# A graph layer on one core: only the source table is made ahead of the edge loop, and node sums move into one tile per batch

## The chip, the cores and the metric

The kernel runs on one core of a Trainium2 chip. The metric is the device time of one execution in microseconds (us); smaller is better. Times of one profiled execution and times of three executions without the profile are given separately, since they differ here.

## The reference

A graph has N = 6250 nodes with 128 features each and E = 100000 edges with 4 attributes each. The edges are sorted by destination. For every edge a small network makes a message; the messages are added up per destination node; a second network updates the nodes; two normalizations follow.

```python
msg_in = concat([x[src], x[dst], edge_attr], axis=1)         # E x 260
h = silu(msg_in @ mW1 + mb1)                                  # E x 128
messages = h @ mW2 + mb2
aggregated = segment_sum(messages, dst, num_segments=N)       # N x 128
u = silu(concat([x, aggregated], axis=1) @ uW1 + ub1)
y = x + (u @ uW2 + ub2)
z = x + (layer_norm(y) * ln_g + ln_b)
out = (z - mean(z)) / sqrt(var(z) + 1e-5)                     # N x 128, float32
```

## The kernel before, in words

**The algebra.** `mW1` has three parts: for the source's features, for the destination's, and for the attributes. The kernel makes two tables in device memory: `tab_a` = x times the first part, `tab_b` = x times the second part plus `mb1`. For an edge it then only needs a row of `tab_a`, a row of `tab_b` and the product of its attributes. Since `h @ mW2` is linear, the kernel adds up `h` itself per node (`acc`, turned: 128 features on the partitions, nodes along the columns) and counts the edges per node (`deg`). The products with `mW2` and with the second part of `uW1` are merged into one matrix `wc` and one row `bc_row` (`merged`).

**The edge loop.** The 100000 edges are cut into 98 groups of 1024, that is eight tiles of 128 edges (the last has six). For group `g`:

- `fetch(g + 4)` issues eight gathers on GpSimd (L159). Each brings 128 rows of `tab_a`, chosen by a list of sources, into a tile `ga`; six such tiles exist. The first five groups (`RAW = 5`) gather from x itself, since `tab_a` is not there yet; for them TensorE turns the rows and multiplies them with the weight in the loop.
- `load(g + 3)` issues three loads on SyncE's queue: the destinations, copied to as many partitions as the window has nodes (`near`, L298), the window of `tab_b` that starts at the group's first destination (`mv`, L414), and the attributes (`st`, L415). The start of the window is a register value.
- `hidden(g)`: VectorE adds `ga` and the product `pre` (L470); ScalarE takes silu into `h` (L471).
- `matrices(g + 2)`: VectorE makes the two one-hot matrices between edges and the 96 nodes of the window (L423, L433).
- `sums(g)`: TensorE multiplies `h` by the one-hot matrix, eight tiles into one PSUM tile `pt` (L479).
- `before_rows(g + 2)`: TensorE makes `pre` out of `mv` and `st` (L455).
- `add(g)`: VectorE adds the 96 columns to `acc` and `deg` at a register's column (L485).

**The nodes.** There are 49 tiles of 128 nodes, in 13 batches of up to four. Because the edges are sorted, a batch's sums are complete some groups after its own. `node_stage` therefore lays the work of one batch over three groups: `node_u` (TensorE, L505 to L507; ScalarE, L509), `node_y` (TensorE, L518 and L519; VectorE, L521 with moments L498 and L499), and `inverse`, `node_z`, `node_o` (ScalarE, L526 and L535; VectorE, L527 to L550; the store, L559). Batch 11 is treated as a whole at group 96, and batch 12, with one tile, after the loop.

**The start.** All of x is loaded into `x_sb`. `turned` (TensorE L319, ScalarE L320) turns a batch into `xT`; `product` multiplies it with both parts of the weight at once (TensorE, L329), ScalarE copies the half for `tab_a` (L331, store L332), VectorE adds `mb1` to the half for `tab_b` (L334, store L335). Between two batches the code places the lists: `destination_lists` turns the destinations and finds each group's first one, and checks that every group fits into its window; if one does not, a general path (`general`, `update`) does the whole work again after the loop. `source_lists` turns the sources into columns for the gathers.

**Order.** The order of instructions on each engine is the order of the code (`manual_schedule`). Waits between engines come from tiles: a new tile of a pool waits until the old tile in its buffer was read.

Of the kernel before, what the change touches and what calls it, by code (L numbers as in the profile page):

```python
# [24 lines left out]
def kernel(  # L25
# [28 lines left out]
    W = 96  # L54
    NW = NP + W
    K1 = W + ED
# [10 lines left out]
    BN = 4  # L67
    NB = -(-NT // BN)
# [3 lines left out]
    assert NG - 2 == (NB - 2) * G + G and NG % RB == 0 and EC * NC == E and EJ * EQ == EC and SQ * SK == NG * G  # L72
# [7 lines left out]
    def tiles_of(g):  # L80
        return min(G, TI - g * G)

# [11 lines left out]
    ps1 = edges.enter_context(tc.tile_pool(name="one_ps", bufs=1, space=PSUM))  # L94

# [3 lines left out]
    def narrow():  # L99
        return ps.tile([P, 2 * P], F32, name="pt")  # L100

    src_l = work.tile([P, GE], I32, name="near")[:SQ, : SK * P].rearrange("q (k c) -> q k c", c=P)
# [3 lines left out]
    x_sb = consts.tile([P, NT, H], F32, name="x_sb")  # L106
    nf = N // P
    w1 = consts.tile([P, 2, H], F32, name="w1")

    def load_x(eng, i0, n):  # L110
        eng.dma_start(
            x_sb[:, i0 : i0 + n, :], x[i0 * P : (i0 + n) * P].rearrange("(i p) c -> p i c", p=P)
        )

    load_x(nc.scalar, 0, 4)
    load_x(nc.sync, 4, 4)
    nc.scalar.dma_start(w1, mW1[: 2 * H].rearrange("(s k) f -> k s f", k=P))
    load_x(nc.sync, 8, 8)
    load_x(nc.scalar, 16, 8)
    load_x(nc.sync, 24, 8)  # L120
    load_x(nc.scalar, 32, 8)
    load_x(nc.sync, 40, nf - 40)
# [3 lines left out]
    w_row_i = consts.tile([P, W], I32, name="w_row_i")  # L126
    nc.gpsimd.iota(w_row_i, pattern=[[1, W]], base=0, channel_multiplier=0)
    p_col_i = consts.tile([P, 1], I32, name="p_col_i")
    nc.gpsimd.iota(p_col_i, pattern=[[0, 1]], base=0, channel_multiplier=1)
    floor_i = consts.tile([1, NB * G], I32, name="floor_i")  # L130
    nc.gpsimd.iota(floor_i, pattern=[[BN * P, NB], [0, G]], base=0, channel_multiplier=0)
# [4 lines left out]
    def source_lists(k0, k1):  # L136
        n = k1 - k0
        src_n = work.tile([P, GE], F32, name="s")[:SQ, : SK * P].rearrange("q (k c) -> q k c", c=P)
        nc.vector.tensor_copy(src_n[:, :n], src_l[:, k0:k1])
        pt = wide()  # L140
        for k in range(n):
            nc.tensor.transpose(pt[:, k, :SQ], src_n[:, k, :], ident[:SQ, :SQ])
        nc.vector.tensor_copy(
            src_s[:, k0 * SQ : k1 * SQ].rearrange("c (k q) -> c k q", q=SQ), pt[:, :n, :SQ]
        )
# [20 lines left out]
    for g in range(RAW):  # L166
        fetch(g)

    if N % P:
        nc.vector.memset(x_sb[:, nf, :], 0.0)  # L170
        nc.sync.dma_start(x_sb[: N - nf * P, nf, :], x[nf * P :])
    nc.vector.memset(src_l[:, SK - 1, :], 0)
    kf = (nf_e - SQ) // SQ
    nc.sync.dma_start(
        src_l[:, 1 : 1 + kf, :],
        src[SQ * P : (1 + kf) * SQ * P].rearrange("(k p c) -> p k c", p=SQ, c=P),
    )
    q0 = nf_e - (1 + kf) * SQ
    if q0:
        nc.sync.dma_start(  # L180
            src_l[:q0, SK - 1, :],
            src[(1 + kf) * SQ * P : nf_e * P].rearrange("(p c) -> p c", c=P),
        )
    if E % P:
        nc.sync.dma_start(
            src_l[q0 : q0 + 1, SK - 1, : E - nf_e * P],
            src[nf_e * P :].rearrange("(o c) -> o c", o=1),
        )
    b1 = bcast("b1", mb1)

    dst_l = work.tile([P, GE], I32, name="near")
# [14 lines left out]
    mv = []  # L206
    for k in range(NM):
        t = consts.tile([K1, H], F32, name=f"mv{k}")
        nc.sync.dma_start(t[W:], mW1[2 * H :])
        mv.append(t)  # L210

    const_ps = ps1.tile([P, W], F32, name="w_row")
    nc.vector.tensor_copy(const_ps, w_row_i)
    w_row = const_ps
# [8 lines left out]

    acc = consts.tile([P, NW], F32, name="acc")
    deg = consts.tile([1, NW], F32, name="deg")
    deg_g = consts.tile([W, NG], F32, name="deg_g")

    def clear():
        for i0, n in groups(NW, NW // 4):
            nc.scalar.copy(acc[:, i0 : i0 + n], zero.to_broadcast([P, n]))  # L230
            nc.scalar.copy(deg[:, i0 : i0 + n], zero[0:1].to_broadcast([1, n]))
# [3 lines left out]
    base_i = consts.tile([1, NG], I32, name="base_i")  # L235
    bad_i = consts.tile([1, 1], I32, name="bad_i")
# [6 lines left out]
    def destination_lists():  # L243
        base_c = work.tile([NG, 1], F32, name="base_c", bufs=1)
        nc.vector.tensor_copy(base_c, dst_l[:, 0:1])
        rel_n = work.tile([P, GE], F32, name="s")[:NG]
# [5 lines left out]
        base_f = work.tile([1, NG], F32, name="base_f", bufs=1)  # L252
        row = to_row(base_c, NG)
        nc.vector.tensor_copy(base_f, row)
        nc.vector.tensor_copy(base_i, row)
        p_b = narrow()
        nc.tensor.matmul(p_b[:, :NG], ones[0:1, :], base_f, start=True, stop=True)
        nc.vector.tensor_scalar(base_p, p_b[:, :NG], p_col, None, op0=OP.add)

        far = work.tile([NG, 2], F32, name="far", bufs=1)  # L260
# [6 lines left out]
        worst = work.tile([1, 2], F32, name="worst", bufs=1)  # L267
        nc.vector.tensor_reduce(worst[:, 0:1], to_row(far[:, 0:1], NG), AX.X, OP.max)
        nc.vector.tensor_scalar(worst[:, 0:1], worst[:, 0:1], -mid * mid, None, op0=OP.add)
        early = work.tile([1, NG], F32, name="early", bufs=1)  # L270
        nc.vector.tensor_copy(early, floor_i[:, :NG])
        nc.vector.tensor_sub(early[:, : NG - 1], early[:, : NG - 1], base_f[:, 1:])
        nc.vector.tensor_reduce(worst[:, 1:2], early[:, : NG - 1], AX.X, OP.max)
# [29 lines left out]
    xT = consts.tile([P, NP], F32, name="xT")  # L303

# [3 lines left out]
    if True:  # L308
        zeros = node.tile([W, H], F32, name="y", bufs=1)
        nc.vector.memset(zeros, 0.0)  # L310
        pad = node.tile([ED, NG * GE - E], F32, name="uT", bufs=1)
        nc.vector.memset(pad, 0.0)
        parts = groups(NT, BN)

        def turned(k):
            i0, n = parts[k]
            pt = wide()
            for i in range(n):
                nc.tensor.transpose(pt[:, i, :], x_sb[:, i0 + i, :], ident)  # L319
            nc.scalar.copy(  # L320
                xT[:, i0 * P : (i0 + n) * P], pt[:, :n, :].rearrange("p i f -> p (i f)")
            )

        def product(k):
            i0, n = parts[k]
            pm = wide().rearrange("p i f -> p (i f)").rearrange("p (i s f) -> p i s f", s=2, f=H)
            for i in range(n):
                cols = slice((i0 + i) * P, (i0 + i + 1) * P)
                nc.tensor.matmul(pm[:, i], xT[:, cols], w1, start=True, stop=True)  # L329
            ta = work.tile([P, G, H], F32, name="s")  # L330
            nc.scalar.copy(ta[:, :n], pm[:, :n, 0])  # L331
            nc.sync.dma_start(by_node(tab_a)[:, i0 : i0 + n, :], ta[:, :n])  # L332
            tb = node.tile([P, BN, H], F32, name="o")
            nc.vector.tensor_add(tb[:, :n], pm[:, :n, 1], b1[:, None, :].to_broadcast([P, n, H]))  # L334
            nc.sync.dma_start(by_node(tab_b)[:, i0 : i0 + n, :], tb[:, :n])  # L335

        turned(0)
        for k in range(len(parts)):
            if k + 1 < len(parts):
                turned(k + 1)  # L340
            product(k)
            if k == 3:
                attributes(0)
            if k == 5:
                destination_lists()
# [236 lines left out]
    for g in range(NG):  # L582
        if g == 3:
            weights()
        if g == 6:
            merged()
# [281 lines left out]
```

## Time and profile before

| what | us |
|---|---|
| median of three executions | 1401.74 (1395.29 to 1404.93) |
| the profiled execution | 1054.17 |
| its span, from the first to the last instruction | 1052.3 |
| GpSimd (POOL) busy in it | 739.4 |
| TensorE (PE) busy | 685.3 |
| VectorE (DVE) busy | 458.5 |
| ScalarE (ACT) busy | 227.3 |

The mean clock that TensorE was granted in the span was 0.734 of full speed. The profile comes from one execution. Its page has the busy time of each engine, a picture of the span in 40 slices, and the costliest groups of instructions. A line such as "L159 POOL DMA_INDIRECT ga<-tab_a,src_i x742 | 700.1, 944 | 250.2 <-issue 206.3" reads: line 159, on POOL, an indirect transfer into the tile `ga`, 742 times, 700.1 us in sum, 944 ns each; POOL stood idle for 250.2 us just ahead of them, of which 206.3 without any wait that the profile shows. PEld is TensorE's weight load. SPq and ACTq are the queues on which SyncE and ScalarE issue transfers.

### The profile page before, as it was taken

The page shows a single profiled execution, that of the slowest core. Times are in us where ns is not written, and L with a number is a line of the kernel's source. Part 1 is how long each engine was busy: PE and PEld are TensorE (multiplying, and loading weights), DVE is VectorE, ACT ScalarE, POOL GpSimd, SP SyncE. Part 2 cuts the span into 40 slices and gives each one's busy share as a digit, 9 for nine tenths or more (in the row PEclk, how much of TensorE's full clock was granted, in tenths as well). Part 3 has the DMA queues.
Part 4 walks back from the last instruction along what each step waited for, and adds up shares of the span by engine and source line. Part 5 has one row for each costly group of instructions (what it writes and reads, how often), then busy time and mean ns, then how long its engine had stood idle before and what let it go on. Part 6 is the DMA issues. An engine that isn't in the chain of part 4 may idle for free. (4 is left out here: it accounts for less than half of the span.)

```text
span 1052.3 us, 11528 instructions
## 1 busy us (share of the span) xinstructions
PE 685.3 (65%) x3791; PEld 605.0 (57%) x3791; DVE 458.5 (44%) x913; ACT 227.3 (22%) x298; POOL 739.4 (70%) x791
## 2 busy tenths in 40 slices
PE   3667884876765775775675575675676675676652
PEld 2447864755755655755665555665566665556631
DVE  1325444736346345335335445435435435335312
ACT  1144112222122122122113122112112112113022
POOL 6707777777777777777777777777777777777710
PEclk7798995977677668668678676667866677766555
DMA  8555542525324324334324325324424433324200
GB/s 214 167 168 139 142 129 75 153 78 145 105 71 139 112 70 134 95 95 132 112 71 139 104 71 145 101 74 127 110 84 129 106 88 116 105 88 116 66 22 15
DMA packets 80699, 114.49 MB, mean 109 GB/s; under 512 B 20791, under 2 KB 58222, under 8 KB 80632
## 3 DMA queue, kind: packets, MB, share of 16 engines
q1 hardware_dynamic: 52728, 60.94, 19.8%
q0 software_dynamic: 25024, 51.30, 17.9%
q10 hardware_dynamic: 2880, 1.44, 0.5%
q8 instruction: 32, 0.52, 0.2%
q14 instruction: 35, 0.29, 0.1%
HBM read 102.34 MB, written 11.28 MB: 108 GB/s over the span
## 5 line engine op out<-in xcount | busy, mean ns | idle before, releaser
L159 POOL DMA_INDIRECT ga<-tab_a,src_i x742 | 700.1, 944 | 250.2 <-issue 206.3
L479 PE MATMUL pt<-oh,h 128*128 128x96 f32 x1564 | 292.0, 363 | 313.0 <-ACT h L471 307.2
L479 PEld LDWEIGHTS pt<-oh,h 128*128 128x128 f32 x1564 | 271.4, 269 | 344.6 <-ACT h L471 337.4
L455 PE MATMUL pre<-mv,st 100*128 100x128 f32 x1564 | 266.3, 337 | 6.6 <-DVE s L446 6.6
L455 PEld LDWEIGHTS pre<-mv,st 100*128 100x128 f32 x1564 | 256.0, 253 | 6.8 <-DVE s L446 6.8
L471 ACT ACTIVATE h<-s 128x1024 f32<-128x1024 f32 (+1 forms) x93 | 98.0, 1053 | 563.4 <-DVE s L470 559.4
L470 DVE TENSOR_TENSOR s<-ga,pre 128x1024 f32<-128x1024 f32 (+1 forms) x93 | 113.3, 1218 | 161.4 <-DMA ga<-tab_a,src_i 152.8
L485 DVE TENSOR_TENSOR acc<-acc,pt 128x96 f32 x98 | 24.9, 254 | 251.1 <-PE pt L479 242.6
L423 DVE TENSOR_SCALAR_CACHE_REDUCE st<-near,base_p 96x1024 f32<-96x1024 int32 x98 | 124.4, 1269 | 3.3 <-issue 3.0
L433 DVE TENSOR_TENSOR oh<-w_row,rel 128x768 f32<-128x768 f32 x98 | 92.8, 947 | 0.0
L159 POOL DMA_INDIRECT ga<-in_x_dram,src_i x40 | 38.1, 953 | 14.3 <-issue 11.9
L521 DVE TENSOR_TENSOR y<-pn,x_sb 128x512 f32<-128x512 f32 (+1 forms) x13 | 8.6, 661 | 79.4 <-PE pn L519 79.4
L329 PE MATMUL pre<-w,xT 128*128 128x256 f32 x98 | 29.7, 457 | 7.3 <-ACT xT L320 5.8
L509 ACT ACTIVATE uT<-pn,ub_col 128x512 f32<-128x512 f32 (+1 forms) x13 | 8.6, 662 | 113.5 <-PE pn L507 113.5
L535 ACT ACTIVATE pn<-y,r 128x128 f32<-128x128 f32 x49 | 22.6, 461 | 35.5 <-DVE r L528 34.3
L334 DVE TENSOR_TENSOR o<-pre,b 128x512 f32<-128x512 f32 (+1 forms) x13 | 8.4, 659 | 48.0 <-ACT s L331 30.6
L329 PEld LDWEIGHTS pre<-w,xT 128*128 128x128 f32 x98 | 21.4, 229 | 13.5 <-ACT xT L320 8.3
L519 PE MATMUL pn<-u,uT 128*128 128x128 f32 x98 | 26.7, 359 | 0.0
L518 PE MATMUL pn<-ub_row,ones 1*128 1x128 f32 x98 | 25.6, 343 | 1.2 <-ACT uT L509 1.2
L477 PE MATMUL pt<-ident,deg_g 96*1 96x96 f32 x98 | 26.1, 266 | 0.0
L485 DVE TENSOR_TENSOR deg<-deg,pt 1x96 f32 x98 | 23.0, 235 | 0.2 <-issue 0.2
L518 PEld LDWEIGHTS pn<-ub_row,ones 1*128 1x128 f32 x98 | 15.6, 198 | 9.2 <-ACT uT L509 3.1
(96 smaller groups left out, 352.5 us busy)
## 6 DMA issues: line engine op xcount, KB each, us to landing
near<-in_dst_dram SPq DMA_DIRECT2D x98, 384.0 KB
ga<-tab_a,src_i POOLq DMA_INDIRECT x742
mv<-tab_b SPq DMA_DIRECT2D x98, 48.0 KB
tab_a<-s SPq DMA_DIRECT2D x12, 256.0 KB
tab_b<-o SPq DMA_DIRECT2D x12, 256.0 KB
out_dram<-o SPq DMA_DIRECT2D x12, 256.0 KB
st<-ea_d SPq DMA_DIRECT2D x98, 16.0 KB
ea_l<-in_edge_attr_dram SPq DMA_DIRECT2D x10, 156.2 KB
```

Of the source, the lines that this page charges most:

```text
L159: nc.gpsimd.indirect_dma_start(out=rows[g][:, i, :], out_offset=None, in_=x if g < RAW else tab_a[:, :], in_offset=bass.IndirectOffsetOnAx ...
L329: nc.tensor.matmul(pm[:, i], xT[:, cols], w1, start=True, stop=True)
L423: nc.vector.tensor_scalar(stbuf[g % NST][:W], near.pop(g), base_p[:W, g : g + 1], 0.0, op0=OP.is_equal, op1=OP.add, accum_out=deg_g[:, g : ...
L433: nc.vector.tensor_tensor(oh[g][:, :n], w_row[:, None, :].to_broadcast([P, n, W]), rel[:, g, :n, None].to_broadcast([P, n, W]), op=OP.is_e ...
L455: nc.tensor.matmul(pre[g][:, i, :], st[:, i, :], mv[g % NM], start=True, stop=not raw)
L470: nc.vector.tensor_add(s[:, :n], rows.pop(g)[:, :n], p[:, :n])
L471: nc.scalar.activation(h[:, :n], s[:, :n], AF.Silu)
L477: nc.tensor.transpose(pt[0:1, P : P + W], deg_g[:, g : g + 1], ident[:W, :W])
L479: nc.tensor.matmul(pt[:, :W], h[:, i, :], o[:, i, :], start=i == 0, stop=i == n - 1)
L485: nc.vector.tensor_add(at, at, of)
L518: nc.tensor.matmul(py[:, i, :], ones[0:1, :], ub2_row, start=True, stop=False)
L519: nc.tensor.matmul(py[:, i, :], u[:, i, :], u2, start=False, stop=True)
```

## The change

- Ahead of the loop only `tab_a` is made, and copied by VectorE (`make_a`). The columns of x, the products for `tab_b` and its rows are made batch by batch in the loop (`load_x`, `turned_x`, `make_b` in `node_stage`), each a group apart; only batches 0 and 1 of `tab_b` come ahead of it. x lives in tiles per batch.
- The lists, the tail of the source lists and the loads of the attribute weights are placed behind the making of `tab_a`; `checks` and the rest of the source lists come at group 6.
- The window has 80 nodes, not 96.
- `acc` and `deg` are tiles of 768 columns per batch. `open_batch` copies what reaches into the next batch and zeroes the rest, on ScalarE. A second register gives the column (`offs`).
- The last two batches have three and two tiles, not four and one; their groups are 94 and 97.
- `before_rows` runs one group ahead, before `sums`. The sum of `ga` and `pre` is made in `ga`. `pt` has one PSUM buffer, not two; one bank `pn` serves the nodes, `turned_x` and `make_b`.
- `node_y` adds the bias row in one product of up to 512 columns, not one per tile. The root's table is loaded early for the last batch.

```diff
-    W = 96
+    W = 80
+    AW = 768
...
+    batches = [(BN * k, BN) for k in range(NT // BN - 1)]
+    rest_t = NT - BN * len(batches)
+    batches += [(NT - rest_t, rest_t - 2), (NT - 2, 2)]
+    NB = len(batches)
+    last = [G * k + G for k in range(NB - 2)] + [NG - 4, NG - 1]
...
     def narrow():
-        return ps.tile([P, 2 * P], F32, name="pt")
+        return ps1.tile([P, 2 * P], F32, name="pt")
+
+    def bank():
+        return ps1.tile([P, BN, P], F32, name="pn")
...
+    def turned_x(k, pt, pool, **kw):
+        n = batches[k][1]
+        for i in range(n):
+            nc.tensor.transpose(pt[:, i, :], xs[k][:, i, :], ident)
+        xT[k] = pool.tile([P, BN * P], F32, **kw)
+        nc.scalar.copy(xT[k][:, : n * P], pt[:, :n, :].rearrange("p i f -> p (i f)"))
...
+    def make_b(k):
+        i0, n = batches[k]
+        pm = bank()
+        product(k, 1, pm)
+        tb = node.tile([P, BN, H], F32, name="o")
+        nc.vector.tensor_add(tb[:, :n], pm[:, :n], b1[:, None, :].to_broadcast([P, n, H]))
+        nc.sync.dma_start(by_node(tab_b)[:, i0 : i0 + n, :], tb[:, :n])
+
+    def make_a(k, pm):
+        i0, n = batches[k]
+        product(k, 0, pm)
+        ta = first.tile([P, BN, H], F32, name="ta", bufs=3)
+        nc.vector.tensor_copy(ta[:, :n], pm[:, :n])
+        nc.sync.dma_start(by_node(tab_a)[:, i0 : i0 + n, :], ta[:, :n])
...
+    for k in range(NB):
+        if k + 1 < NB:
+            pt[k + 1] = turned_first(k + 1)
+        make_a(k, pt.pop(k)[:, BN:])
...
+    lists = destination_lists()
+    make_b(0)
+    make_b(1)
...
-        s = work.tile([P, G, H], F32, name="s")
-        nc.vector.tensor_add(s[:, :n], rows.pop(g)[:, :n], p[:, :n])
+        s = rows.pop(g)
+        nc.vector.tensor_add(s[:, :n], s[:, :n], p[:, :n])
         nc.scalar.activation(h[:, :n], s[:, :n], AF.Silu)
...
+    def open_batch(k):
+        acc[k] = node.tile([P, AW], F32, name="acc")
+        deg[k] = node.tile([1, AW], F32, name="deg")
+        c0 = 0
+        if k:
+            width = batches[k - 1][1] * P
+            c0 = AW - width
+            nc.scalar.copy(acc[k][:, :c0], acc[k - 1][:, width:])
+            nc.scalar.copy(deg[k][:, :c0], deg[k - 1][:, width:])
+        nc.scalar.copy(acc[k][:, c0:], zero.to_broadcast([P, AW - c0]))
+        nc.scalar.copy(deg[k][:, c0:], zero[0:1].to_broadcast([1, AW - c0]))
...
     def node_stage(g):
...
+        for k in range(NB - 1):
+            if g == last[k]:
+                node_u(k)
...
+        for k in range(2, NB):
+            if g == G * k - G - 2:
+                load_x(nc.sync, k, node, name="x", bufs=3)
+            if g == G * k - G - 1:
+                turned_x(k, bank(), node, name="xT", bufs=3)
+            if g == G * k - G:
+                make_b(k)
...
         if g == 6:
-            merged()
+            checks(*lists)
+            source_lists(1, SK)
+            start.close()
...
-        pt = sums(g)
-        if g == RAW - 1:
+        if g + 1 >= RAW:
             before_rows(g + 1)
-        if g >= RAW - 1:
-            before_rows(g + 2)
-        add(g, pt)
+        if g == NG - 1:
+            node_x(NB - 1)
+        add(g, sums(g))
         node_stage(g)
```

## The prediction

> **What bounds the kernel now.** I read the page's table of busy time first, then POOL's waits, then the timeline at the head, at a batch in the middle and at the tail. The page's groups give the pace:
>
> ```profile
> PE 685.3 (65%) x3791; PEld 605.0 (57%) x3791; DVE 458.5 (44%) x913; ACT 227.3 (22%) x298; POOL 739.4 (70%) x791
> ...
> L159 POOL DMA_INDIRECT ga<-tab_a,src_i x742 | 700.1, 944 | 250.2 <-issue 206.3
> ```
>
> No engine is full: POOL is busy 70%. But its idle time is mostly "issue", which is no wait. The waits of POOL show how it splits:
>
> ```profile
> POOL ga L159 <- issue: 218.2, 716, 0.3
> POOL ga L159 <- DMA ea_d<-uT: 24.3, 1, 24.3
> POOL ga L159 <- DMA ga<-tab_a,src_i: 12.5, 41, 0.3
> ```
>
> The columns are total, times and longest. Hundreds of pauses of 0.3 us, none longer, and one of 24.3 us. A gather of 128 rows so costs 0.944 + 0.305 = 1.249 us, whatever else runs, and the 782 gathers of the kernel take 782 x 1.249 = 977 us of the 1052.3 us span. Everything in the loop has to beat eight gathers, 10.0 us per group; if it does, it is free. The timeline (start, duration, engine, line) shows the two ends that POOL does not fill:
>
> ```profile
> 4.14 1.11 POOL L159 DMA_INDIRECT ga<-in_x_dram,src_i  x1 [2.38 <-DVE near L172]
> ...
> 53.20 0.94 POOL L159 DMA_INDIRECT ga<-in_x_dram,src_i  x1 [0.30 <-issue]
> ...
> 76.70 0.32 SPq L353 DMA_DIRECT2D ea_d<-uT  x1
> ...
> 78.44 0.94 POOL L159 DMA_INDIRECT ga<-tab_a,src_i  x1 [24.30 <-DMA ea_d<-uT]
> ...
> 1003.45 0.94 POOL L159 DMA_INDIRECT ga<-tab_a,src_i  x1 [0.30 <-issue]
> ...
> 1029.51 0.95 DVE L470 TENSOR_TENSOR s<-ga,pre 128x768 f32<-128x768 f32 x1
> ...
> 1033.28 2.88 PE L479 MATMUL pt<-oh,h 128*128 128x96 f32 x12 [15.13 <-ACT h L471]
> ...
> 1046.46 0.26 SPq L563 DMA_DIRECT2D out_dram<-o  x1
> ```
>
> The 40 gathers from x end at 54.1. The next needs tab_a, whose last write goes out at 75.1, in one queue with tab_b's, so POOL stands until 78.4 (the named ea_d is merely the last DMA of that queue). At the end POOL is done at 1004.4, and 47.9 us follow. The last group's rows are there by about 1007, but its add starts at 1029.5: batch 11 is ahead of it on DVE and ACT.
>
> Is the loop really below 10 us? Windows of 80 us, eight groups each, say so for the busy sums (columns PE, PEld, DVE, ACT, POOL; PE has 48 to 56 of 80 us in three of them):
>
> ```profile
> 564.00:644.00 80.00, 51.27 (x302) 46.07 (x302) 38.35 (x74) 16.29 (x22) 60.45 (x65) 0.76 0.36 104
> ```
>
> At the lower PE clock it is tight. From the tail's rows: sums 3.73, pre 3.67, a small transpose 0.37, so 7.8 per group, 62 per eight; batch matmuls add 6.1 (L505 to L507) and 6.4 (L518, L519): 75 of 80 us.
>
> **What the Trainium skill says.** "Perfetto Trace Analysis", per-instruction lifecycle: a gather's row ends when its descriptors are written, not when data land. It agrees: group 96's last gather ends at 996.9 and its add, which waited for it, starts at 999.4, so landing costs 2.5 us. "DMA: Bandwidth & Descriptors", SWDGE vs HWDGE vs iDMA: cores of GpSimd compute these descriptors in software. The trace agrees, 940 to 961 ns over 742 gathers, so smaller loads elsewhere shall not quicken them. "TensorE: Matmul & The Clock Gate", Part 1: the PE clock is either half or full. The same sums take 2.02 and 3.73 us here. "Runtime: NRT & Kernel Launch", model-switch cost, gives about 70 us for a first execution: no cover for the gap in the next part.
>
> **The two times.** The profiled execution took 1054.2 us, the median of the runs is 1401.7: 347 us that no view shows. If they are a constant around the kernel, an edit's gain carries over unchanged. If each gather is slower without the profile, they are 0.44 us on each of 782. If all is slower alike, it is a factor 1.33. I work in the profiled execution and carry the difference over unchanged, the middle of the three.
>
> **The change, part by part.**
>
> *Head.* Tables are made in 13 steps. Before, a step is four transposes (0.60), four products of 256 columns (1.99) and an ACT copy (0.58): starts 3.2 us apart. Now products have 128 columns (1.0 to 1.7), and one DVE copy (about 0.66) frees the buffer: 2.4 to 3.2 us. Three further costs of before go: b1's late landing (DVE waits 17.4 us, to 23.7), the destination lists between steps 5 and 6 (PE's next transposes start at 48.3 instead of near 40) and source lists (2 us). But the queue of SP carries six x tiles, b1 and three lists ahead of the first tab_a write, and the copy tiles are three deep, so step 3 waits for write 0, issued by my estimate at 18 to 20 us. Then 10 steps x 2.4 to 3.2, and 2.5 to land: tab_a is ready at 45 to 55, against 54.1 when POOL asks, plus two iotas of 0.25. I take 1 us of wait left and 0.6 of iotas: 24.3 - 1.6 = 22.7 gained.
>
> *What is late next.* The lists, tab_b's first two batches and the four mv loads now come after A, and the loop starts behind them. On SP: last tab_a write about 52, src lists and mv loads (these four took 4.3 before) to 57, tab_b to 60, the register load 2.3, mv landed at 65.5. On DVE two matrices (2.2 each) and two copies of 1.2 follow, so the first sums come near 78 to 81, against 89.85 before. Raw groups take 7.6 us each (89.85, 97.44, 105.08), so the activation of group 5 ends near 114 to 118. This matters since it now releases the gather's buffer (the sum is made in place, until now DVE's add released it): six buffers, so gather group 11, due at 54.9 + 60 = 115, waits for it. At g = 6 DVE runs checks and source_lists first (two reduces of 1.21, ten of about 0.2, casts of 0.55 and 0.86, some 7 us), and group 12 waits for that: 0 to 7 us in all, I take 3. Head: 19.7 gained.
>
> *Loop.* Windows of 80: the largest distance inside a group in the reference's dst is 70 nodes and offsets reach 529 of 688, so the general path stays unused. Sums lose 16 of 96 columns (3.73 to 3.1), oh 16% of 0.95, near 64 KB. Added per eight groups: four transposes (1.1 slow), four products (3.3), a DVE add (0.69), one x load and a tab_b write on SP. node_y's four bias matmuls become one of 512 columns (3.2 to 2.07). open_batch is four ACT copies (0.4 to 0.7 each, 2.2) ahead of uT. There is one pn bank, so make_b on PE waits for uT, about 2.7, and behind PE wait pre and the next sums. Slow PE: 8 x 7.2 = 57 + 6.1 + 5.3 + 4.4 + 2.7 = 76 of 80, one more than before. Both hide behind the gathers: zero. Without that cover, one microsecond per batch costs 11. make_b's write also sits in SP's queue ahead of the next near, mv and st; it delays them up to 9 us, and near(g+4) has nearly two groups, so zero.
>
> *Tail.* From POOL's end E (1004.4 there): y of batch 11 (three tiles) delays the add of group 96 from E-5 to E-2.6; activation to E-1.5, sums E+1.7, inverse and z of batch 11 on DVE to E+7. Then group 97: add 0.95, activation 0.9, sums 2.4, add 0.5, two matmuls of 256 columns 2.2, silu 0.5, y 2.8, add and moments 1.5, root and reciprocal 0.9, scaling 1.0, three DVE operations 1.4, moments 1.0, inverse 0.8, scaling 1.0: 17.9, so E+24.9. From the last ACT (1046.4) to the end before: 5.9. Sum 30.8 against 47.9: 17.1 gained. Of this 8 come from batch 11 done sooner, the rest from the shorter queue in front of group 97.
>
> Total 19.7 + 17.1 = 37 us, to a span of 1015; the median becomes 1402 - 37 = 1365.
>
> **Rivals.** *The missing 347 us are in the gathers* (0.20). 40 raw gathers then end at 72, not 54, and only 6 of the 24.3 us were ever waited for; the gain is 5 + 17 = 22, so 1380. For it: gathers are most of the time. Against: their spread is 2%. *Everything is slower alike* (0.08): 37 x 1.33 = 49, 1353. *A still comes late* (0.12): SP's queue and landing x tiles keep tab_a until 70, and the lists' wait comes at 7: gain 24.3 - 16 - 7 + 17 = 18, so 1384. *The batch work makes the loop the bound* (0.10, slower): place, the group where node_u, open_batch, uT and make_b run in turn through one pn bank; PE there waits for ACT and ACT for DVE. Price: what an eight-group stretch takes beyond 80 us, times 11. It decides from 84 on (4 saved, 3.4 break even). If waits of 2 to 3 us come at each of node_u, make_b, node_y and z, 76 becomes 85 to 86, so 11 x 5.5 = 60 - 37: 1425. For it: 76 of 80 at the slow clock. Against: the clock was full in part of every window (0.69 to 0.76 on average).
>
> **How the numbers follow.** The forecast has 0.50 and by its own costs 1350 to 1375. Leaving out the slower rival and the upper edge of the late table gives 1340 to 1395. A measurement here tells about 1% (14 us) from none: faster from 1388 down. Faster: 0.48 + 0.17 + 0.08 + 0.08 = 0.81; same 0.10; slower 0.09.
>
> **What would show it.** Right: POOL's wait for a DMA on tab_a below 5 us, waits for ACT of a few us near 115 to 130, pauses of 0.3 elsewhere, 31 us after the last gather. Wrong: a wait of POOL for ACT in every eighth group, or a gather pitch other than 1.25 us.

## The result, and the profile after

| | median, us | runs |
|---|---|---|
| the kernel before | 1403.34 (1395.29 to 1412.18) | 4 |
| the changed kernel | 1453.05 (1446.99 to 1463.32) | 4 |
| ratio | 1.036, 95% interval 1.027 to 1.045 | |

The forecast was 1365 us with a range of 1340 to 1395. The change is 50 us slower in this comparison instead of 37 us faster.

The profiled execution of the changed kernel took 1463.32 us, and its span 1461.5. So nothing large lies outside of the span here, as it had seemed to in the profile of the kernel before (1054.17 profiled, 1401.74 as median). First the page of the changed kernel: TensorE's busy time, its clock in 40 slices, and two groups (sum and mean of their busy time, then the idle time ahead of them and what ended most of it):

```profile
PE 885.3 (61%) x3858; PEld 777.7 (53%) x3858; DVE 451.3 (31%) x936; ACT 238.8 (16%) x338; POOL 739.3 (51%) x792
...
PEclk9987756556555555555555555555555555555555
...
L181 POOL DMA_INDIRECT ga<-tab_a,src_i x742 | 699.9, 943 | 638.5 <-ACT h L516 372.1
...
L545 DVE TENSOR_TENSOR acc<-acc,pt 128x80 f32 x98 | 23.4, 238 | 733.1 <-remote 504.1
```

The gathers cost what they cost before (943 ns), but POOL now stands for 638.5 us ahead of them, 372.1 of it until ScalarE has read the gather's buffer. The add of the sums (L545) stands 504.1 us for "remote", a release that the profile can put down to no instruction. The waits (total, times, longest) show how few and how long these are:

```profile
ACT h L516 <- DVE ga L515: 541.1, 55, 21.2
DVE acc L545 <- remote: 504.1, 35, 15.5
POOL ga L181 <- ACT h L516: 372.1, 53, 15.6
...
POOL ga L181 <- DMA src_l<-in_src_dram: 38.9, 1, 38.9
```

Thirty-five waits of 14.4 us on average, in 98 groups. And the wait for `tab_a`, which was to fall from 24.3 us to 1.6, is 38.9. Two groups on the timeline (start, duration, engine, line), TensorE first and then the adds of the sums on VectorE:

```profile
751.36 3.70 PE L524 MATMUL pt<-oh,h 128*128 128x80 f32 x16 [2.30 <-ACT h L516]
754.86 3.70 PE L500 MATMUL pre<-mv,st 84*128 84x128 f32 x16
758.35 0.34 PE L522 MATMUL pt<-ident,deg_g 80*1 80x80 f32 x1
758.48 3.62 PE L524 MATMUL pt<-oh,h 128*128 128x80 f32 x16
761.90 3.70 PE L500 MATMUL pre<-mv,st 84*128 84x128 f32 x16
774.62 0.29 PE L522 MATMUL pt<-ident,deg_g 80*1 80x80 f32 x1 [9.02 <-DVE deg L545]
```

```profile
755.10 0.24 DVE L545 TENSOR_TENSOR acc<-acc,pt 128x80 f32 x1 [3.08 <-PE pt L524]
...
774.19 0.24 DVE L545 TENSOR_TENSOR acc<-acc,pt 128x80 f32 x1 [15.41 <-remote]
```

The first group's sums are recorded to 755.06, and VectorE adds them at 755.10. The second group's are recorded to 762.10, but VectorE gets them at 774.19, 12 us later. The semaphore events of the trace say the same: one for the first `pre` at 761.47, where the record ends at 758.56; then one at 774.17 for the second group's sums and one at 774.33 for its `pre`. So the results of 33 instructions took 12.9 us to come, 0.39 us for each on average, and the records give them about 7 us. It is no even pace: the first group's 16 matmuls were done in the 3.7 us that their record says. "Perfetto Trace Analysis" of the Trainium skill, section Tensor Engine Instruction, says that the profiler works out the end of a TensorE instruction from its size and does not observe it. This trace agrees: the end of the second group's sums is 12 us too early, and only whoever waits for the result shows it.

### The profile page after: what moved, and what is told of

Same layout as the page of the kernel before. It is cut to its first block, busy times and chain, and to the rows that moved or that the text cites. A ratio compares the mean times of both kernels' runs of the same rounds, so it can differ in the third digit from the quotient of the medians.

```text
span 1461.5 us, 12138 instructions
## 1 busy us (share of the span) xinstructions
PE 885.3 (61%) x3858; PEld 777.7 (53%) x3858; DVE 451.3 (31%) x936; ACT 238.8 (16%) x338; POOL 739.3 (51%) x792
## 4 chain that ended last, share of the span: by engine, by line
another core or an unknown queue 37%; PE 25%; DVE 16%; issue 12%; ACT 5%; DVEq 2%; DMA 1%; POOL 1%; ACTq 0%; SPq 0%
PE pt L524 12%; PE pre L500 4%; DVE ga L515 4%; DVE st L468 4%; ACT h L516 3%; DVE oh L478 2%; PE pn L569 2%; PE pn L570 2%; ACT pn L597 2%; DVE bn L556 1%; PE pn L328 1%; DVE var L557 1%; PE pre L328 1%; DVEq L515 1%
## 5 line engine op out<-in xcount | busy, mean ns | idle before, releaser
L181 POOL DMA_INDIRECT ga<-tab_a,src_i x742 | 699.9, 943 | 638.5 <-ACT h L516 372.1
L524 PE MATMUL pt<-oh,h 128*128 128x80 f32 x1564 | 348.1, 415 | 174.6 <-ACT h L516 156.8
L524 PEld LDWEIGHTS pt<-oh,h 128*128 128x128 f32 x1564 | 332.8, 323 | 194.9 <-ACT h L516 172.2
L500 PE MATMUL pre<-mv,st 84*128 84x128 f32 x1564 | 351.0, 409 | 23.1 <-issue 22.1
L500 PEld LDWEIGHTS pre<-mv,st 84*128 84x128 f32 x1564 | 332.4, 318 | 28.3 <-issue 27.0
L545 DVE TENSOR_TENSOR acc<-acc,pt 128x80 f32 x98 | 23.4, 238 | 733.1 <-remote 504.1
L516 ACT ACTIVATE h<-ga 128x1024 f32<-128x1024 f32 (+1 forms) x93 | 98.1, 1055 | 726.2 <-DVE ga L515 541.1
L522 PE MATMUL pt<-ident,deg_g 80*1 80x80 f32 x98 | 30.9, 315 | 191.6 <-DVE deg L545 191.6
L468 DVE TENSOR_SCALAR_CACHE_REDUCE st<-near,base_p 80x1024 f32<-80x1024 int32 x98 | 124.3, 1269 | 7.1 <-issue 5.2
L515 DVE TENSOR_TENSOR ga<-ga,pre 128x1024 f32<-128x1024 f32 (+1 forms) x93 | 113.2, 1217 | 26.8 <-issue 22.0
L478 DVE TENSOR_TENSOR oh<-w_row,rel 128x640 f32<-128x640 f32 x98 | 79.8, 814 | 0.0
L569 PE MATMUL pn<-acc,wc 128*128 128x512 f32 (+2 forms) x26 | 24.3, 1037 | 89.2 <-DVE acc L545 89.2
L328 PEld LDWEIGHTS pn<-w,xT 128*128 128x128 f32 x98 | 20.2, 305 | 25.6 <-ACT uT L572 22.7
```

The costliest lines, as they stand in the source:

```text
L181: nc.gpsimd.indirect_dma_start(out=rows[g][:, i, :], out_offset=None, in_=x if g < RAW else tab_a[:, :], in_offset=bass.IndirectOffsetOnAx ...
L328: nc.tensor.matmul(pm[:, i, :], xT[k][:, i * P : (i + 1) * P], w1[:, part, :], start=True, stop=True)
L468: nc.vector.tensor_scalar(stbuf[g % NST][:W], near.pop(g), base_p[:W, g : g + 1], 0.0, op0=OP.is_equal, op1=OP.add, accum_out=deg_g[:, g : ...
L478: nc.vector.tensor_tensor(oh[g][:, :n], w_row[:, None, :].to_broadcast([P, n, W]), rel[:, g, :n, None].to_broadcast([P, n, W]), op=OP.is_e ...
L500: nc.tensor.matmul(pre[g][:, i, :], st[:, i, :], mv[g % NM], start=True, stop=not raw)
L515: nc.vector.tensor_add(s[:, :n], s[:, :n], p[:, :n])
```

## The experiments

The chips on which the runs took place are of two kinds. On kind A (four chips) the kernel before takes 1048 to 1054 us, on kind B (four others) 1394 to 1423, profiled or not. All runs of one chip are compared with runs of the kernel before on the same chip, so ratios are used below, with the kind beside them. In the first comparison the kernel before took 1403 us, kind B. No run shows one of these chips at two different times, so whether the kind belongs to a chip for good or to its state at that hour is not shown.

The theories, as the expectations name them. R: in some executions TensorE's results come late, and this bounds the loop. O: the missing 347 us lie outside of the span or evenly everywhere. Q: the one buffer of `pt` makes TensorE's queue stop, and that makes results late. S: the new order of `before_rows` does it. L: late results belong to the chip and strike any kernel. W: groups of 80 nodes keep TensorE at half clock. C and K: of these, the columns of the sums or the rows of the other matmul decide. T: on kind B, TensorE's own pace per instruction bounds the loop.

### Where are the 347 us, and is it the buffer or the order?

before_again is the kernel before, unedited.

> The kernel before, unchanged, for a second trace. Theory R (late results): in the executions that are timed, results of TensorE reach VectorE up to 12 us after the records of the matmuls end, as in the trace of the changed kernel; expects about 1400 us inside the span, gaps of 8 to 12 us before the adds of L485, PE clock about 0.55. Rival O (outside): the 347 us lie outside the span; expects a span near 1052 us with pauses of POOL of 0.3 us only.

1052.84 us, seven further runs 1048.24 to 1052.08 (kind A). On this chip there are no 347 us at all, in or outside of the span (1051.1).

e1 gives the second buffer back:

```diff
-        return ps1.tile([P, 2 * P], F32, name="pt")
+        return ps.tile([P, 2 * P], F32, name="pt")
```

> The changed kernel with two PSUM buffers for pt, as before. Theory Q (queue stops): with one buffer the transpose of the next group's degrees waits for VectorE's add, PE's queue stands, and the results come late; expects the waits of PE L522 for DVE (191.6 us) to go and 1453 to fall to 1400 or below. Rival S (order): it is the place of before_rows ahead of sums that matters; expects no change, 1440 to 1465.

e2 keeps one buffer and restores the order of before, with the rest of the source lists four groups earlier:

```diff
-        if g + 1 >= RAW:
-            before_rows(g + 1)
...
-        add(g, sums(g))
+        pt = sums(g)
+        if g == RAW - 1:
+            before_rows(g + 1)
+        if g >= RAW - 1:
+            before_rows(g + 2)
+        add(g, pt)
```

> The changed kernel with before_rows two groups ahead and behind sums, as before (the rest of the source lists moves from group 6 to group 2 to make room), pt still with one buffer. Theory S (order) expects 1400 or below; theory Q expects 1440 to 1465.

e3 has both edits.

> Both: pt with two buffers and before_rows as before. If the loss of the change is in the hand-over between PE and DVE and the rest of the prediction holds (head 20 us, tail 17 us gained), about 1365; if what costs is the batch work that now stands in the loop (x, turning, table B, opening of batches), still 1440 or more.

Ratios on kind A: e1 0.972 (0.968 to 0.975), e2 1.071 (1.067 to 1.074), e3 1.074 (1.072 to 1.076). Expected times near 1365 or 1440 us don't apply, since the chip was of the other kind. In no trace of these was a result of TensorE late, so R could not be seen in them. The old order is dear here, with one buffer as with two; why, e7 shows.

### The changed kernel itself on kind A, and the width

after_again is the changed kernel, unedited.

> The changed kernel, not edited, beside the kernel before on one chip. In its first comparison both were slow (1453 against 1403 us), and TensorE's results came 9 to 12 us late in 35 of its 98 groups; the kernel before has since taken 1049 us. Theory L (the late results belong to the condition of that chip, and strike any kernel there): no late result here, and a time near the one with two buffers of pt, 1015 to 1050 us, a ratio of 0.97 to 1.00. Theory Q (the single buffer of pt makes TensorE's queue stop and the results late by itself): the ratio stays near 1.036 or above, with waits of the sums' add of 9 to 12 us.

1027.87 us against 1050.57: ratio 0.976 (0.972 to 0.981). The same program that is 3.6% slower on kind B is 2.4% faster on kind A, and no result is late (of 351 signals of TensorE, none comes over 1 us after its record ends). e1's interval overlaps with this one: the second buffer is worth nothing that shows. L holds: the late results go with the chip. Q has nothing to stand on here.

e4 is e1 with 96 nodes per group, e5 the kernel before with 80:

```diff
-    W = 80
+    W = 96
```

> The changed kernel with two buffers of pt and 96 nodes per group instead of 80. Theory W (the narrow groups, 84 rows and 80 columns instead of 100 and 96, keep TensorE at half clock): the granted clock goes from 0.575 back to 0.70 or more and the 1564 matmuls of the rows before the activation from 411 ns to about 345. Rival (the order of the work on TensorE or its longer waits keep the clock low): the clock stays below 0.60 and the sums' matmuls cost more, 430 ns or over. Gathers bound both, so the time lies at 1015 to 1035 us if W holds and at 1030 to 1060 us under the rival.

> The kernel before with 80 nodes per group and nothing else. Theory W: the granted clock falls from 0.73 to below 0.62 and the matmuls of both loops cost over 400 ns each, although each has less to do; the time goes up by 0 to 7%, to 1050 to 1125 us, according to how much room the gathers leave. Rival: the clock stays at 0.70 or above, the matmuls get cheaper, and the time is 1040 to 1050 us.

e4: 0.966 (0.963 to 0.969), e5: 1.030 (1.026 to 1.033). The clock in 40 slices, and the groups of TensorE, of before_again and then e5:

```profile
PEclk8798996968678577677677687766767667576655
...
L479 PE MATMUL pt<-oh,h 128*128 128x96 f32 x1564 | 297.4, 368 | 301.6 <-ACT h L471 296.0
L455 PE MATMUL pre<-mv,st 100*128 100x128 f32 x1564 | 272.2, 342 | 6.6 <-DVE s L446 6.6
```

```profile
PEclk8698955555555555555555555555555555555555
...
L479 PE MATMUL pt<-oh,h 128*128 128x80 f32 x1564 | 346.2, 413 | 168.9 <-ACT h L471 163.2
L455 PE MATMUL pre<-mv,st 84*128 84x128 f32 x1564 | 356.3, 416 | 5.8 <-DVE s L446 5.8
```

One number is changed, W. Each matmul has less to do and takes longer: 413 for 368 ns, 416 for 342. The slices show why: after the head the clock never leaves its half. W holds. (These means are recorded durations, of overlapping instructions. The adds of the sums agree: from 250 us to the last gather they come every 10.13 us in e5, every 9.88 in before_again.) A group then takes a little longer than its eight gathers, 10.0 us, and the lag shows at the end: the gathers' part of the loop is only 2.9 us longer (928.9 against 925.9), while from the last gather to the end it is 77.2 us against 47.4.

e6 is the kernel before with one buffer of `pt`.

> The kernel before with one buffer of pt instead of two, and nothing else. Theory Q: the degree's transposition now waits for the add of the group before, TensorE's queue stands, and the time goes up by 1% or more (1060 us or over). Rival (the add is done long before the next group's sums are due, since the rows of two groups ahead stand between them): within 0.5% of 1049 us.

1.001 (0.999 to 1.003), kind A. The buffer costs nothing there.

e7 is e3 at 96 nodes, e8 the changed kernel at 96 nodes and nothing else.

> The kernel with two buffers of pt and with the rows of two groups ahead in the order of the kernel before (1127 us at 80 nodes per group), now at 96 nodes per group. Theory W (half clock is what makes that order dear: at 80 nodes each matmul of both loops takes 416 ns, and a group's node products stand behind 16 of them): clock 0.70 or more, at most 20 us of POOL's waits for the activation (62.6 at 80 nodes), time 1020 to 1050 us. Rival (the order itself is dear, since products of the batch stand behind the rows of two groups ahead): 1080 us or over at whatever clock.

> The changed kernel at 96 nodes per group, with its one buffer of pt. If the one buffer costs nothing where TensorE's results come in time, as the comparison of 1028 us (one) with 1028 us (two) at 80 nodes suggests, this is within 5 us of the 1016 us that two buffers gave at 96 nodes, at a clock of 0.70 or more. If the single buffer does cost something that the half clock hid, it is 1022 us or over. On a chip where results come late (the kernel before near 1400 us), the clock theory says that width alone brings it below the kernel before; theory Q says that it stays above.

e7: 0.972 (0.968 to 0.975), e8: 0.967 (0.961 to 0.973), both kind A. The order that cost 7% at 80 nodes costs little at 96 (0.972 with it, 0.966 without it in e4), so it is dear together with half clock alone. And e8, 1013.93 us, is one number away from the changed kernel: its ratio is the lower one, though the two intervals touch (at 0.972), and that of e4 doesn't. POOL's waits in after_again, then in e8:

```profile
POOL ga L181 <- issue: 229.2, 731, 6.7
POOL ga L181 <- ACT h L516: 13.9, 3, 6.0
```

```profile
POOL ga L181 <- issue: 219.3, 720, 0.3
POOL ga L181 <- DMA ga<-tab_a,src_i: 14.3, 47, 0.3
POOL ga L181 <- DVE src_i L165: 2.6, 1, 2.6
```

In after_again POOL waits three times for a buffer, 13.9 us, and 6.7 us (the longest "issue") ahead of its first gather of `tab_a`. In e8 nothing longer than 2.6 us is left: POOL is the bound from the first gather to the last. But these two traces lie further apart than the two kernels do: that of after_again is of the slowest of its four executions (1032.87), that of e8 of the fastest (1012.24). The wait ahead of `tab_a` is not a matter of the width: it is 5.0 us in e4, at 96 nodes, and 0.3 in e10, at 80. For the buffers, e1 and e4 compare well, since their first gathers of `tab_a` start equally late (59.7 and 59.5): 17.6 us at 80 nodes, 5.9 at 96, in one execution each.

e9 widens only the one-hot matrix of the sums to 96 columns, e10 only the other matmul to 100 rows, by 16 rows of zeros.

> The changed kernel with 80 nodes per group, but with 96 columns in the one-hot matrix of the sums (16 columns that no edge meets): the matmul of the sums again has 96 columns, the rows' matmul stays at 84 rows. Theory C (the columns of the sums decide what clock is granted): clock 0.70 or more and 1010 to 1022 us, like the width of 96 as a whole. Rival K (the 84 rows of the other matmul decide): clock below 0.62 and 1022 to 1045 us, since each of the sums' matmuls has more to do at half clock.

> The changed kernel with 80 nodes per group, but with 16 rows of zeros added to the rows' matmul, so that it has 100 rows again; the sums' matmul keeps its 80 columns. Theory C (the columns of the sums decide the granted clock): clock below 0.62 and 1022 to 1040 us, as without the edit. Rival K (the rows decide): clock 0.70 or more, 1010 to 1022 us.

e9 met kind B: 1.039 (1.033 to 1.044), clock 0.59, and tells nothing of the clock on kind A. e10 (A): 0.970 (0.965 to 0.975), clock 0.64 to 0.67, where the changed kernel has 0.57 to 0.60 and e8 0.75 to 0.77. The rows are a part of it and not the whole; what the columns do stays open.

### Kind B

before_4th is the kernel before once more, for its trace.

> The kernel before, not edited, for its trace. If it takes about 1050 us, it shows again that TensorE's results come in time there (at most 2 of 300 late by over 1 us). If it takes about 1400 us, theory R says that the 350 us lie in waits of VectorE for late results of TensorE (8 to 16 us each, in 25 to 35 of the 98 groups), as in the changed kernel's first trace; rival O says that they lie at no one place, with every group longer by the same 3.5 us.

1410.67 us, span 1408.8: kind B. Its waits:

```profile
DVE acc L485 <- remote: 484.2, 34, 26.1
...
POOL ga L159 <- DVE s L470: 317.1, 55, 10.1
...
POOL ga L159 <- DMA ea_d<-uT: 52.4, 1, 52.4
```

and two groups of it, TensorE and then the adds:

```profile
728.24 1.98 PE L479 MATMUL pt<-oh,h 128*128 128x96 f32 x16
730.06 1.98 PE L455 MATMUL pre<-mv,st 100*128 100x128 f32 x16
731.88 0.25 PE L477 MATMUL pt<-ident,deg_g 96*1 96x96 f32 x1
```

```profile
724.86 0.25 DVE L485 TENSOR_TENSOR acc<-acc,pt 128x96 f32 x1 [2.91 <-PE pt L479]
742.68 0.26 DVE L485 TENSOR_TENSOR acc<-acc,pt 128x96 f32 x1 [13.98 <-remote]
```

The late results are there without the change: 34 waits, 484 us, against 35 and 504. That is where the 347 us lie, and inside of the span. R holds and O falls. Note the rows of TensorE: recorded at full clock, 32 matmuls in 3.8 us, done by 732.04; the result arrives at 742.66. From the signal ahead of these 33 instructions (729.92) to that of their last (742.82) it is 12.9 us, the same as in the changed kernel, where the records had half clock. The records give no hint of that pace.

e11 is e8's kernel, on kind B.

> The changed kernel at 96 nodes per group once more. Where the kernel before takes 1050 us: 1010 to 1022 us, as before. Where it takes 1400 us: theory W alone (half clock is all that makes the change slower there) gives a ratio below 0.99; theory R (there the late results bound the loop, whatever the clock) gives 1.02 to 1.05, like the 1.036 and 1.039 of 80 nodes.

On the chip of before_4th it takes 1494.56 us, 1.058 (1.054 to 1.062), at a clock of 0.664, where the kernel before has 0.66. So half clock isn't what makes the change slower on kind B. It is even slower at 96 nodes there than at 80, beyond what R expected (1.02 to 1.05).

e13 is e1's kernel on kind B; e12 is the changed kernel with fewer matmuls for the batches:

```diff
-        for i in range(n):
+        for i in range(1 if one else n):
             nc.tensor.transpose(pt[:, i, :], xs[k][:, i, :], ident)
...
-        nc.vector.tensor_add(tb[:, :n], pm[:, :n], b1[:, None, :].to_broadcast([P, n, H]))
+        nc.vector.tensor_add(tb[:, :n], pm[:, 0:1, :].to_broadcast([P, n, H]), b1[:, None, :].to_broadcast([P, n, H]))
```

> The changed kernel, but in the loop only one of the up to four transpositions of a batch of x and one of the up to four matmuls of its B are done, and the one result is spread over the batch: 69 of the matmuls in the loop are left out (so the values of B and of the turned x are not those of the reference), while copies, adds and DMAs stay. Where the kernel before takes 1050 us: the half clock leaves TensorE so little room in the batches' groups that the waits after them shrink, 1015 to 1028 us. Where it takes 1400 us: theory T (TensorE's own pace, about 0.4 us for a matmul there, bounds the loop, and the batch's matmuls lengthen it) gives 25 us or more off 1453, a ratio of 1.02 or below; theory R alone (the late results come by the group, whatever else TensorE has to do) leaves the ratio at 1.03 or above.

> The changed kernel with two buffers of pt once more. Where the kernel before takes 1050 us: 1020 to 1035 us as before. Where it takes 1400 us: theory Q (the one buffer makes TensorE's queue stop, and that makes the results late) gives a ratio of 1.01 or below; its rival (the queue then stops at the next wait, for the activation, as in the kernel before with its two buffers) leaves 1.03 or above.

The count of 69 was off: it is 66 matmuls and transpositions, six of them ahead of the loop. The page counts a product as two instructions: 3756 instead of 3858, 90 fewer in the loop. e13: 1.032 (1.023 to 1.041), 36 late waits. Q falls. e12, on the same chip: 1.011 (1.006 to 1.016), 42 us less than e13. (The two differ in `pt` as well, but e13's ratio is that of the changed kernel within the noise.) The adds' waits of e12, then e13:

```profile
DVE acc L549 <- remote: 458.8, 32, 15.5
```

```profile
DVE acc L545 <- remote: 520.4, 36, 15.5
```

From the first gather of `tab_a` to the last gather e13 takes 1306.9 us, e12 1261.2: 45.7 us for 90 instructions.

e14 takes out transpositions alone and leaves nothing out: the turned x stays in SBUF from its first turning.

```diff
-            turned_x(k, pt, first, name="xT", bufs=2)
+        turned_x(k, pt, kept, name=f"xT{k}")
...
-            if g == G * k - G - 1:
-                turned_x(k, bank(), node, name="xT", bufs=3)
```

> The changed kernel, but the turned x of all batches stays in SBUF from the first turning, so that the 41 transpositions of the loop and their copies go; nothing is left out of the result. Where the kernel before takes 1400 us, theory T (about 0.4 us of TensorE for each of its instructions in the loop) gives 41 x 0.4 = 16 us less than the change, a ratio of 1.02 to 1.03; rival (the batch's products of B and their wait for uT in the one pn bank make up what e12 saved) leaves it at 1.033 or above. Where it takes 1050 us: 1015 to 1028 us.

e15 is e5's kernel, on kind B.

> The kernel before at 80 nodes per group once more, 1.030 where the kernel before takes 1050 us, since TensorE is then granted half clock. Where it takes 1400 us, theory T (the loop goes at TensorE's own pace there, whatever clock the records show, and 80 columns are less work than 96) gives a ratio of 0.97 to 0.99, as the change at 80 (1.036) stands to the change at 96 (1.058); theory W (the clock decides there too) gives 1.01 or above.

e14: 1425.60 us, 1.018 (1.011 to 1.025), half of the loss gone for 41 instructions fewer (3817), a little more than T expected. That is 0.018 x 1403 = 25 us, 0.6 us for each (by the ends of the two intervals, on two chips, anything from 3 to 47 us); e12's are 0.5. Both are above the mean of 0.39. The waits and copies that go with the instructions can be the rest; no run parts them. e15: 1.029 (1.023 to 1.034). Here T's expectation of 0.97 to 0.99 is wrong: less work per matmul is no gain to the kernel before. Together with e11 (96 nodes slower in the changed kernel) the width is not understood on kind B. Other parts of the change were not undone there: the order of `before_rows`, the sum in place, and ScalarE's copies in `open_batch`.

## Why the prediction was wrong, point by point

**The step that failed.** "Both hide behind the gathers: zero": the loop's added work was given no price, because the profile had eight gathers as the bound of every group. On kind B, in before_4th and in the profile after, late results of TensorE bound the loop, and it became 64.8 us longer. The way there was the choice on the two times. The prediction saw 347 us that no view shows, named three readings, and chose to "carry the difference over unchanged, the middle of the three". In truth the profile was taken where TensorE's results come in time, and the times, by their size (1395 to 1405 us, as on kind B), where they don't. These are two different bounds, so no constant and no factor carries one over to the other. None of the three readings (constant, gathers, all alike) said that the bound itself is another.

**What bounds the kernel.** "Everything in the loop has to beat eight gathers, 10.0 us per group; if it does, it is free" holds on kind A. On kind B, from the first add after 250 us to the last before the gathers end, before_4th takes 13.36 us per group and the changed kernel 14.02. Divided by TensorE's instructions in that stretch it is 0.374 and 0.388 us for each, 0.382 to 0.386 in e12, e13 and e14, but 0.403 in e11. In the two kernels and e8 on kind A it is 0.26 to 0.28, and POOL bounds. So on kind B TensorE's work is on the path.

**The sum on kind B.** Spans 1408.8 (before_4th) and 1461.5, on two chips:

```profile
106.50 0.94 POOL L159 DMA_INDIRECT ga<-tab_a,src_i  x1 [52.42 <-DMA ea_d<-uT]
...
1340.27 0.94 POOL L159 DMA_INDIRECT ga<-tab_a,src_i  x1 [0.30 <-issue]
```

```profile
93.11 0.94 POOL L181 DMA_INDIRECT ga<-tab_a,src_i  x1 [38.89 <-DMA src_l<-in_src_dram]
...
1391.68 0.94 POOL L181 DMA_INDIRECT ga<-tab_a,src_i  x1 [0.30 <-issue]
```

Head: 13.4 us earlier. Loop, from there to the end of the last gather: 1234.7 to 1299.5, 64.8 more. Tail: 67.6 to 68.9, 1.3 more. Sum 52.7. In this stretch the traces have 3420 instructions of TensorE before and 3520 after: 41 transpositions and 98 instructions of B come in, with some 27 of other kinds that stood ahead of it, and 66 of the bias row go out. An estimate from the mean pace is 100 x 0.39 = 39 us of the 64.8. The rest is not explained: each instruction takes longer on average (0.388 for 0.374), and why is open. e12 and e14 show that the added instructions, with the waits that go with them, matter by more than the estimate says. The tail's gain is gone: the changed kernel has 69 us after the last gather here, and 29 on kind A.

**Head.** On kind A the wait for `tab_a` fell from 23.6 to 6.7 us, and to 0.3 in e8. From before_again to e8 the first gather of `tab_a` moves from 77.7 to 55.0, by 22.7 us. That this is the number of the prediction to the digit is luck: after_again's comes at 61.1, 16.6 us earlier than before, and what delays it is not shown. The mechanism was right. "What is late next" was priced at 3 us of buffer waits: they are 13.9 in after_again and 0.6 in e8.

**Loop.** "Slow PE: 76 of 80, one more than before ... zero" holds on kind A, though at 80 nodes it is half clock nearly all along and not the mixture of before. The loop of after_again is 14.7 us longer than that of before_again (940.7 against 925.9; 926.2 in e8), and nearly all of it lies in three waits near its start:

```profile
123.72 0.94 POOL L181 DMA_INDIRECT ga<-tab_a,src_i  x1 [2.94 <-ACT h L516]
...
139.40 0.94 POOL L181 DMA_INDIRECT ga<-tab_a,src_i  x1 [5.99 <-ACT h L516]
...
194.15 0.94 POOL L181 DMA_INDIRECT ga<-tab_a,src_i  x1 [5.02 <-ACT h L516]
```

They are the first gathers of groups 11, 12 and 17. Groups 11 and 12 are the ones that "what is late next" named. Later POOL waits for no buffer, at the same half clock: from 250 us on a group takes 9.57 us, less than its gathers. The edit "windows of 80" was costed as a pure saving ("3.73 to 3.1") and is a term that was mis-signed. The sums of 80 columns are recorded with 3.62 to 3.70 us at half clock, and full clock, which does them in 2.02 at 96, is hardly granted any more. By the ratios it takes back about 9 us of the changed kernel on kind A (0.976 at 80 nodes, 0.967 at 96, intervals that touch; 14 us between the medians), and 3% of the kernel before. The Trainium skill, "TensorE: Matmul & The Clock Gate", Part 1, section What's actually happening, has full clock after about 3.4 us of sustained work. This case differs, as far as its records tell. TensorE in the timeline of after_again:

```profile
644.01 3.62 PE L524 MATMUL pt<-oh,h 128*128 128x80 f32 x16
647.43 3.70 PE L500 MATMUL pre<-mv,st 84*128 84x128 f32 x16
650.92 0.34 PE L522 MATMUL pt<-ident,deg_g 80*1 80x80 f32 x1
651.05 3.62 PE L524 MATMUL pt<-oh,h 128*128 128x80 f32 x16
654.47 3.70 PE L500 MATMUL pre<-mv,st 84*128 84x128 f32 x16
```

Each row starts before the one above ends, for over 14 us, and 16 instructions still take 3.6 to 3.7 us, which before_again has at half clock; at full clock they take 1.98 to 2.02.

**Tail.** Last gather to end on kind A: 47.4 to 29.3, 18.2 gained; predicted 17.1. The mechanism is the predicted one too: the last group's add of rows (L470 before, L515 after) starts 6.1 us after the last gather in after_again, 24.7 in before_again; the forecast was 7.

**The sum on kind A** is 16.6 - 14.7 + 18.2 = 20.1 us of span (1051.1 to 1031.0), and 22.7 between the medians. In e8, without half clock, it is 40.7 in its fastest execution, and 38.5 between the medians. So the mechanism of the head and of the tail was right, and 37 us was about what they give at 96 nodes.

**The rivals.** "The batch work makes the loop the bound" (0.10, forecast slower, 1425) had the direction on kind B, though not the place. Its sign, waits of POOL for ACT, came 53 times and not in every eighth group, and it tells little: before_4th has 55 such waits for its own releaser, L470. e12 left the turns through one `pn` bank in place and still won back most of the loss, so they are not its main part. The point from which it decides, 84 us per eight groups, had long been passed there: 8 x 13.36 = 107 in the kernel before. Slower gathers and "everything slower alike" fall: gathers (943 to 946 ns) and VectorE's 458 us are the same on both kinds. "A still comes late" is near to what kind A shows, with 18 us of gain for the 20.1 that were measured.

## What to carry to other kernels

When a profiled execution and the timed ones differ by a quarter, the gap is the first thing to settle: what hides behind the bound of the profile may be the bound of the times, so an edit that moves work "for nothing" from the head into the loop needs its price under both. A lag of an engine behind the bound can stay hidden in the buffers and come out in the tail, as in e5. On TensorE read the waits of those who use the results, since its own rows are modelled. And narrowing a matmul is not a saving by itself: look at the granted clock of the same kernel at both widths.

## What was not expected of the hardware

- Chips of one type, as they were met here, differ by 34% on the same program (1052 and 1411 us), with the same gathers (943 to 944 ns) and the same recorded durations of the other engines (VectorE 458.3 and 458.2 us busy).
- On kind B 33 instructions of TensorE took 12.9 us, 0.39 us each on average, where the records give 0.12 to 0.23 at a recorded clock of 1.0 or 0.5. The semaphore of the sums came with that of the rows behind them, 0.16 us apart, while the sums of the group before came on time. What holds them is open.
- 84 rows and 80 columns instead of 100 and 96 hold the granted clock at half after the head (kernel before, kind A: mean 0.56 instead of 0.73). With 100 rows and 80 columns it is 0.64 to 0.67.
